# Layers 2 and 3 of a graph network: the row tile that ten blocks share, split once into kept halves

## The chip, the core and the metric

The kernel runs on one core of one Trainium2 chip. The time is the device time of one execution in microseconds (us); lower is better. TensorE is called PE in the views, VectorE DVE, ScalarE ACT, GpSimd POOL, and SyncE SP.

## What is computed

A graph network of 6250 nodes with 256 features and 100,000 edges `src -> dst`, sorted by `dst`. Three layers of the same form, a residual sum and a layer norm:

```
deg  = in-degree + 1 (a self loop on each node);  dinv = 1/sqrt(deg)
for W, b in ((W1, b1), (W2, b2), (W3, b3)):      # 256 -> 512 -> 512 -> 256
    h = relu( segment_sum( (h @ W)[src] * dinv[src] * dinv[dst], dst ) + b )
out  = layernorm(x + h)
```

Each `segment_sum` runs over the edges and the self loops. All data is float32.

## The kernel before, in words

The nodes are cut into 50 blocks of Q = 125. A layer needs, for each block, the sum over its edges of rows of a table (`tab0` for layer 1, `tab1`, 512 wide, for layer 2, `tab2`, 256 wide, for layer 3; they hold the scaled node values and lie in HBM). The code numbers the layers i = 0, 1, 2.

A block's sum is made in one of two ways. A **gathered** block has 16 chunks of 128 edges. For each chunk GpSimd issues an indirect DMA that brings 128 rows of the table into SBUF (line 1159), and PE multiplies them by a 0/1 matrix `shot` that says which row belongs to which node of the block (line 1186). Blocks 22 to 49 are gathered in layer 1, blocks 12 to 49 in layer 2 (38 blocks), blocks 29 to 49 in layer 3 (21 blocks). A **dense** block is made by a product of a matrix of edge counts with the whole table (line 1242 in layers 1 and 3, line 1014 ahead of time; in layer 2 `teams` multiplies four dense blocks at once, line 957).

A block may have more edges than 16 chunks hold. The excess of ten blocks goes into one extra tile of 128 rows, the **shared row tile**, gathered once per ten blocks (the items with `b is None`). Its 17th column of `shot` picks a block's part. So each gathered block ends with a 17th product, of the shared tile, behind its 16th chunk.

For PE, a float32 row tile is split into two halves of the type float32r: ACT copies the row (line 1213, the high half), DVE subtracts the copy from the row (line 1216, what is left), and PE multiplies both. In layer 2 a half is 512 columns, so a chunk is two products of 512 columns; in layer 3 a half is 256 columns, the two lie side by side, and a chunk is one product of 512 columns. The shared tile is not split: it is multiplied as float32 in every block. `product` (lines 1162 to 1196) issues these; the list `several` holds the chunk's halves and, at the block's last chunk, the shared tile from `of_ten`.

The order is written out by hand (`tc.manual_schedule()`), one pass of the loop at line 1203 per chunk. In pass `chunk` stand: the gather of `chunk` (line 1208), ACT's copy of chunk - `hi_lag`, DVE's subtraction of chunk - `lo_lag`, the product of chunk - `lag`, then steps of what follows a block (`after1`, `after2`, `after3`), then dense work. `SPLIT` (line 54) sets the lags: 1, 2 and 8 passes in layer 2, 3, 4 and 9 in layer 3. Every engine runs its own list in order, so a wait holds up all that stands behind it on that engine.

Buffers go round in rings. The raw rows of a layer are a list `rows`; its first two are the two shared tiles (line 1141) and the others a ring that the gathers use in turn: 7 in layer 2 (each 128x512), 17 in layer 3. A raw row is free again when DVE has subtracted. The split rows are a queue `split`: 9 of its own in layer 2 and 3 lent ones (`loaned`, which lie in the space of `parts`, so that the trace shows them as `parts`), 11 in layer 3. A split row goes back to the queue when its product stands (line 1192). Near the end of the teams' work the lent ones aren't put back, and `lag` goes down from 8 to 6.

`after2` turns a finished sum of layer 2 into rows of `tab2`: DVE scales the sum (line 1308), PE transposes it, ACT copies it out (line 1326), PE multiplies by W2 (line 1352), ACT applies the bias and relu (line 1363), PE multiplies by W3 (line 1372), DVE scales (line 1385), SP stores into `tab2` (line 1388, through the helper's line 73). This is done for two blocks at a time. Layer 3's first gather needs the last of these stores. In layer 3 the dense counts are fetched from HBM (`fetch`, through the helper's line 75) into the space `room`, of which the first part also holds raw rows of layer 2, the shared ones among them. `after3` adds the bias and x, takes the norm and stores the output.

Of the kernel before, what the change touches and what calls it, by code (L numbers as in the profile page):

```python
# [10 lines left out]
F32 = mybir.dt.float32  # L11
# [21 lines left out]
LATE = 6  # L33
# [362 lines left out]
def sorted_path(ctx: ExitStack, tc: tile.TileContext, x, edges, starts, found, wts, biases, room, late, out):  # L396
# [14 lines left out]
    nc = tc.nc  # L411
# [22 lines left out]
    rest = const.tile([P, NG, 2], I32, name="rest")  # L434
# [313 lines left out]
    def split_rows_of(stack, name, i, width):  # L748

        pool = stack.enter_context(tc.tile_pool(name=name, bufs=1))  # L750
        return deque(pool.tile([P, 2 * width], F32R, name=f"halves{n}") for n in range(SPLIT_ROWS[i]))

    split = split_rows_of(one, "sfirst_split", 0, C)
# [269 lines left out]
    def fetch(b, chunk):  # L1023
        by_rows(nc.sync, used[len(there) % 2].rearrange("p k v -> p (k v)"), kept[b])
        there.append(chunk)
# [5 lines left out]
    def layer(i, width, gathered, dense, after, rows, first=0, spacing=1.0, extras=(), filler=None, carried=None):  # L1031
# [29 lines left out]
        def go_fixed(chunk):  # L1061
            for item in list(fixed):
                if item[0] <= chunk:
                    wait = next(item[1], None)
                    if wait is None:
                        fixed.remove(item)
                    else:
                        item[0] = chunk + wait

        def go(chunk):  # L1070
            for item in list(going):
                if item[0] <= chunk + late:
                    wait = next(item[1], None)
                    if wait is None:
                        going.remove(item)
                    else:
                        item[0] = chunk + late + min(wait, item[2])
# [8 lines left out]
        def sum_bank(name, most):  # L1086
            nonlocal late
            if i == 0:
                while not common:
                    if early_copy[0]():  # L1090
                        break
                    late += 1
                    go(chunk)
                return common.popleft()
            need(now, name, most)
            return idle[name].pop(0)

        def ended(chunk, b, acc, bank="acc"):

            most = LATE if chunk < total - 2 * KF else 1  # L1100
            going.append([chunk + late + min((3, SOON, LATE)[i], most), after(b, acc, bank), most])
            for item in going:
                item[2] = most
# [4 lines left out]
        def more_hots():  # L1108
            c0 = len(hots) * HOTS
            n = min(HOTS, len(gathered) * (KF + 1) - c0)  # L1110
            if n > 0:
                at = gathered[0] * (KF + 1) + c0
                hot = onehot.tile([P, HOTS, Q], F32R, name="shot")
                nc.vector.tensor_tensor(hot[:, :n], near_cols[:, :Q].unsqueeze(1).to_broadcast([P, n, Q]),  # L1114
                                        dlo.rearrange("p b j -> p (b j)")[:, at:at + n].unsqueeze(2).to_broadcast([P, n, Q]),
                                        op=ALU.is_equal)
                hots.append(hot)

        def converted(m, c):
            piece = pieces.tile([Q, PIECE, Q], F32R, name="piece")  # L1120
            convert = nc.vector.tensor_copy if i == 2 and c % 4 == 1 else nc.scalar.copy
            made_or_read = place_of[dense[m]] if i == 0 else used[m % 2] if m else made
            convert(piece, made_or_read[:, c * PIECE:(c + 1) * PIECE, :])  # L1123
            return piece
# [5 lines left out]
        def of_both(c):  # L1130

            n, b, _ = items[c]
            return i == 0 and (n * GRP if b is None else b) >= BOTH_FROM

        def halved(c):

            return 0 <= c < total and items[c][1] is not None and i > 0
        acc = None

        of_ten = {}  # L1140
        shared, rows = rows[:2], rows[2:]

        def gather(c):
            nonlocal turn
            n, b, j = items[c]
            table = both_halves if of_both(c) else tables[i]
            if (i, b, j) == (0, BOTH_FROM, BOTH_LAG + 1):
                hot_stores.appendleft(late_hot_room)
            if b is None:
                row, at = split.popleft() if of_both(c) else shared[n % 2], rest[:, n, 0:1]  # L1150
                of_ten[n] = row
            elif of_both(c):
                row, at = split.popleft(), src[:, b, j:j + 1]
                split_rows[c] = row
            else:
                row, at = rows[turn % len(rows)], src[:, b, j:j + 1]
                (landed if i > 0 else split_rows)[c] = row
                turn += 1
            nc.gpsimd.indirect_dma_start(out=row, out_offset=None, in_=table,  # L1159
                                         in_offset=bass.IndirectOffsetOnAxis(ap=at, axis=0))  # L1160
# [39 lines left out]
        with tc.manual_schedule():  # L1200
            more_hots()
            to_sum = 0
            for chunk in range(total + (SHORT if i == 1 else lag)):
                now = chunk
                if i == 1:
                    lag = SPLIT[i][2] if returning is None else max(SHORT, SPLIT[i][2] - (chunk - returning) // 2)
                if chunk < total:
                    gather(chunk)
                if halved(chunk - hi_lag):
                    halves = split_rows[chunk - hi_lag] = split.popleft()  # L1210
                    if i == 1 and halves in loaned:
                        on_loan.append(halves)
                    nc.scalar.copy(halves[:, :width], landed[chunk - hi_lag])  # L1213
                if halved(chunk - lo_lag):
                    halves = split_rows[chunk - lo_lag]
                    nc.vector.tensor_sub(halves[:, width:], landed.pop(chunk - lo_lag), halves[:, :width].bitcast(F32))  # L1216
                while to_sum <= chunk - lag:
                    product(to_sum)
                    to_sum += 1
                go(chunk)  # L1220
                go_fixed(chunk)
                until = min(len(dense) * NB, begun + int((chunk + 1 - first) * NB / spacing))
                if i == 0:
                    until = min(until, done + 3)
                if chunk >= total - 1:
                    until = len(dense) * NB
                while done < until:
                    m, k = divmod(done, NB)
                    if k == 0:
                        if chunk < total - 1 and (len(there) <= m or there[m] > chunk):  # L1230
                            break
                        assert len(there) > m
                        acc_d = sum_bank(bank, 3)
                        if i == 2 and m + 1 < len(dense) and len(there) == m + 1:
                            fetch(dense[m + 1], chunk)
                    if k % PIECE == 0:
                        while len(got) < min(len(dense) * CUTS, done // PIECE + 1 + ahead):
                            n, c = divmod(len(got), CUTS)
                            if n > m and (len(there) <= n or there[n] > chunk):
                                break  # L1240
                            got.append(converted(n, c))
                    nc.tensor.matmul(acc_d[:Q], lhsT=got[done // PIECE][:, k % PIECE, :], rhs=parts[:, k],  # L1242
                                     start=(k == 0), stop=(k == NB - 1))
                    products = done = done + 1
                    if k == NB - 1:
                        finished += 1
                        ended(chunk, dense[m], acc_d, bank)
            assert all(steps_ is carried for _, steps_ in fixed)
            while going:
                late += 1  # L1250
                go(chunk)
                if carried is not None:
                    next(carried)
                if filler is not None:
                    next(filler, None)
            while filler is not None and begun % PIECE:
                next(filler)
# [214 lines left out]
    split = split_rows_of(two, "swide_split", 1, HID)  # L1472
# [11 lines left out]
    split = split_rows_of(ctx, "ssplit", 2, C)  # L1484
    spacing = (steps(MANY) - 14) / (MANY - begun / NB)
    layer(2, C, every[MANY:], many, after3, last_rows, 4, spacing)


# [179 lines left out]
```

## Time and profile before

| what | value |
|---|---|
| median of 3 runs | 2101.11 us (2099.72 to 2102.96) |
| the profiled execution's own time | 2099.83 us |
| its span, first to last instruction | 2098.2 us |
| mean granted TensorE clock in it | 0.982 |
| HBM read and written | 415.75 MB, 67.46 MB (230 GB/s over the span) |
| layer 1's gathers / layer 2's / layer 3's | 451 / 612 / 339 (1402 indirect DMAs in all; layer 2 and 3 with 4 and 3 shared tiles) |
| first gather of layer 2 / of layer 3 | at 709.2 us / at 1647.2 us of the span |

The durations in the views are of this one execution. A matmul of two float32 operands shows as two MATMUL records, one of float32r operands as one; both print as `f32`. Matmuls overlap in the pipeline, so the time that one costs in a stream is the distance from its start to the next one's start, not its own duration. In the groups of lines a row ends with busy time, mean duration of one and the idle time of the engine just before them.

### The profile page before, as it was taken

The page shows a single profiled execution, that of the slowest core. Times are in us where ns is not written, and L with a number is a line of the kernel's source. Part 1 is how long each engine was busy: PE and PEld are TensorE (multiplying, and loading weights), DVE is VectorE, ACT ScalarE, POOL GpSimd, SP SyncE. Part 2 cuts the span into 40 slices and gives each one's busy share as a digit, 9 for nine tenths or more (in the row PEclk, how much of TensorE's full clock was granted, in tenths as well). Part 3 has the DMA queues.
Part 4 walks back from the last instruction along what each step waited for, and adds up shares of the span by engine and source line. Part 5 has one row for each costly group of instructions (what it writes and reads, how often), then busy time and mean ns, then how long its engine had stood idle before and what let it go on. Part 6 is the DMA issues. An engine that isn't in the chain of part 4 may idle for free.

```text
span 2098.2 us, 30149 instructions
## 1 busy us (share of the span) xinstructions
PE 1948.5 (93%) x8711; PEld 1518.5 (72%) x8711; DVE 1492.8 (71%) x2822; ACT 1307.4 (62%) x2497; POOL 1421.2 (68%) x1442
## 2 busy tenths in 40 slices
PE   3499999999998789999999999999989899999997
PEld 3377777777776567878878777788767787887775
DVE  5887888888882466776667776577775367777777
ACT  1566777787784466666667666667565456555554
POOL 2467777766777376767667776577775477777775
PEclk9999999999999899999999999999999999999998
DMA  7797999999999999988889898799886376767674
GB/s 167 238 285 231 267 263 255 276 261 260 270 276 256 266 258 254 273 232 247 236 237 268 255 264 226 219 257 264 248 238 192 103 185 181 192 176 192 175 188 120
DMA packets 232032, 485.37 MB, mean 231 GB/s; under 512 B 42937, under 2 KB 85769, under 8 KB 231857
## 3 DMA queue, kind: packets, MB, share of 16 engines
q0 software_dynamic: 125184, 315.61, 54.2%
q1 hardware_dynamic: 90833, 155.90, 26.7%
q10 hardware_dynamic: 15840, 11.86, 2.3%
q8 instruction: 70, 1.15, 0.2%
q14 instruction: 105, 0.86, 0.1%
HBM read 415.75 MB, written 67.46 MB: 230 GB/s over the span
## 4 chain that ended last, share of the span: by engine, by line
PE 67%; DMA 10%; issue 7%; DVE 5%; POOL 4%; ACT 3%; ACTq 0%; SPq 0%; DVEq 0%; POOLq 0%
PE sacc L1186 14%; DMA room<-tab,ssrc 9%; PE win_ps L1352 6%; PE smm L1242 5%; PE win_ps L1242 5%; PE mat_ps L1242 5%; PE sacc L1242 5%; POOL room L1159 4%; PE win_ps L1372 3%; PE sacc L957 2%; PE mat_ps L957 2%; PE str L957 2%; PE smm L957 2%; PE sacc L1289 2%; PE str L1242 2%
## 5 line engine op out<-in xcount | busy, mean ns | idle before, releaser
L1159 POOL DMA_INDIRECT room<-tab,ssrc x1008 | 1028.3, 1020 | 403.3 <-issue 157.2
L1216 DVE TENSOR_TENSOR halves<-room,halves 128x512 fp32r<-128x512 f32 (+1 forms) x818 | 460.4, 579 | 295.1 <-ACT halves L1213 274.7
L1213 ACT CAST halves<-room 128x512 fp32r<-128x512 f32 (+1 forms) x818 | 417.8, 531 | 299.3 <-DMA room<-tab,ssrc 243.8
L1186 PE MATMUL sacc<-halves,shot 128*125 128x512 f32 x1468 | 509.2, 407 | 11.5 <-DVE shot L1114 5.6
L1159 POOL DMA_INDIRECT halves<-both,ssrc x384 | 360.5, 939 | 141.7 <-issue 42.9
L783 DVE TENSOR_TENSOR room<-near_cols,slots 128x625 bf16<-128x625 f32 (+2 forms) x435 | 324.9, 802 | 28.5 <-PE sacc L850 12.2
L1186 PEld LDWEIGHTS sacc<-halves,shot 128*125 128x125 f32 x1468 | 275.4, 189 | 88.4 <-ACT halves L1213 6.6
L1123 ACT CAST piece<-room 125x625 fp32r<-125x625 uint8 x416 | 297.7, 723 | 65.4 <-DVE halves L1216 26.1
L1114 DVE TENSOR_TENSOR shot<-near_cols,sdlo 128x500 fp32r<-128x500 f32 x371 | 247.3, 667 | 9.7 <-PE sacc L1186 5.2
L1352 PE MATMUL win_ps<-room,w_sb 128*128 128x250 f32 (+1 forms) x832 | 190.1, 371 | 14.0 <-ACT room L1326 6.7
L1242 PE MATMUL win_ps<-parts,piece 125*125 125x512 f32 x650 | 186.8, 406 | 5.0 <-ACT piece L1123 4.9
L1242 PE MATMUL smm<-parts,piece 125*125 125x512 f32 x655 | 190.0, 407 | 1.3 <-ACT piece L1123 0.7
L1352 PEld LDWEIGHTS win_ps<-room,w_sb 128*128 128x128 f32 x832 | 154.5, 192 | 42.1 <-ACT room L1326 8.2
L1242 PE MATMUL mat_ps<-parts,piece 125*125 125x512 f32 x600 | 173.1, 406 | 0.4 <-ACT piece L1123 0.4
L850 PEld LDWEIGHTS <-room 128*125 128x125 bf16 x725 | 95.7, 138 | 73.7 <-issue 22.7
L1242 PE MATMUL sacc<-parts,piece 125*125 125x512 f32 x450 | 146.6, 430 | 0.9 <-ACT piece L1123 0.9
L1242 PEld LDWEIGHTS win_ps<-parts,piece 125*125 125x125 f32 x650 | 119.3, 188 | 35.9 <-ACT piece L1123 6.3
L812 ACT CAST room<-sacc 125x500 uint8<-125x500 f32 (+1 forms) x155 | 107.7, 713 | 51.3 <-PE sacc L850 50.9
L1242 PEld LDWEIGHTS smm<-parts,piece 125*125 125x125 f32 x655 | 116.8, 187 | 29.1 <-issue 2.3
L1242 PEld LDWEIGHTS mat_ps<-parts,piece 125*125 125x125 f32 x600 | 108.0, 187 | 27.2 <-issue 2.8
L919 DVE TENSOR_TENSOR parts<-parts 125x512 fp32r<-125x512 f32 x150 | 103.1, 687 | 33.9 <-ACT parts L917 33.7
L957 PE MATMUL sacc<-parts 125*125 125x512 f32 x300 | 106.0, 433 | 13.4 <-ACT parts L917 11.8
(311 smaller groups left out, 3003.3 us busy)
## 6 DMA issues: line engine op xcount, KB each, us to landing
parts<-tab SPq DMA_DIRECT2D x81, 448.0 KB
kept<-room SPq DMA_DIRECT2D x29, 683.6 KB
room<-kept SPq DMA_DIRECT2D x29, 683.6 KB
room<-tab,ssrc POOLq DMA_INDIRECT x1008
tab<-st SPq DMA_DIRECT2D x62, 224.0 KB
both<-parts SPq DMA_DIRECT2D x10, 1120.0 KB
own_row<-tab SPq DMA_DIRECT2D x38, 224.0 KB
parts<-kept SPq DMA_DIRECT2D x60, 136.7 KB
```

The source lines that it names most:

```text
L783: nc.vector.tensor_tensor(out, near_cols[:, :shape[2]].unsqueeze(1).to_broadcast(shape), numbers.unsqueeze(2).to_broadcast(shape), op=ALU. ...
L812: nc.scalar.copy(place[:, :, u * G:(u + len(ms)) * G].rearrange("p k (t r) -> p t k r", r=G), counted_in[:Q, :len(ms) * 256].rearrange("p ...
L919: nc.vector.tensor_sub(to[:, HID:], row, to[:, :HID].bitcast(F32))
L957: nc.tensor.matmul(team_banks[n][:Q], lhsT=team_pieces[(g * CUTS + k // PIECE) % 2][n][:, k % PIECE, :], rhs=both_parts[u % 3][:, h * HID: ...
L1114: nc.vector.tensor_tensor(hot[:, :n], near_cols[:, :Q].unsqueeze(1).to_broadcast([P, n, Q]), dlo.rearrange("p b j -> p (b j)")[:, at:at + ...
L1123: convert(piece, made_or_read[:, c * PIECE:(c + 1) * PIECE, :])
L1159: nc.gpsimd.indirect_dma_start(out=row, out_offset=None, in_=table, in_offset=bass.IndirectOffsetOnAxis(ap=at, axis=0))
L1186: nc.tensor.matmul(acc[:Q, :size], lhsT=hot, rhs=row[:, c0:c0 + size], start=(i == 1 and k == c0 == 0), stop=(k == KF and c0 + size == row ...
L1213: nc.scalar.copy(halves[:, :width], landed[chunk - hi_lag])
L1216: nc.vector.tensor_sub(halves[:, width:], landed.pop(chunk - lo_lag), halves[:, :width].bitcast(F32))
L1242: nc.tensor.matmul(acc_d[:Q], lhsT=got[done // PIECE][:, k % PIECE, :], rhs=parts[:, k], start=(k == 0), stop=(k == NB - 1))
L1352: nc.tensor.matmul(h_ps[:, f, :], lhsT=w2_sb[:, k, (f2 + f) * P:(f2 + f + 1) * P], rhs=zt2[:, k, :wide], start=(k == 0), stop=(k == KH - 1))
```

## The change

In layers 2 and 3 one raw row is kept for shared tiles where there were two, and the one left over joins the ring of raw rows (8 in layer 2, 18 in layer 3). One split row is taken out of `split` for the length of the layer: `shared_halves`. Once per ten blocks, ACT copies the shared tile into its first half and DVE subtracts into the second, 6 to 8 passes behind the gather of the tile and not before the last product of the ten blocks before it stands. The blocks' 17th products then read `shared_halves`: two float32r products of 512 columns in layer 2, one in layer 3. `product` is unchanged. Layer 1 is unchanged.

```
-        shared, rows = rows[:2], rows[2:]
+        shared, rows = rows[:2 if i == 0 else 1], rows[2 if i == 0 else 1:]
+        shared_halves = split.popleft() if i > 0 else None
+        raw_of_ten = deque()
...
             if b is None:
-                row, at = split.popleft() if of_both(c) else shared[n % 2], rest[:, n, 0:1]
+                row, at = split.popleft() if of_both(c) else shared[n % len(shared)], rest[:, n, 0:1]
                 of_ten[n] = row
+                if i > 0:
+                    of_ten[n] = shared_halves
+                    raw_of_ten.append((c, row))
...
                 while to_sum <= chunk - lag:
                     product(to_sum)
                     to_sum += 1
+                if raw_of_ten and to_sum >= raw_of_ten[0][0] and chunk >= raw_of_ten[0][0] + LATE:
+                    row = raw_of_ten.popleft()[1]
+                    nc.scalar.copy(shared_halves[:, :width], row)
+                    nc.vector.tensor_sub(shared_halves[:, width:], row, shared_halves[:, :width].bitcast(F32))
                 go(chunk)
                 go_fixed(chunk)
```

In the built program the lists of PE, ACT and DVE stand in the same order as before but for the replaced products and the seven added copies and subtractions (four in layer 2, three in layer 3); GpSimd's list is the same. On SP one pair of DMAs moves: near the end of layer 2, a fetch of dense counts (`room<-kept`) stands ahead of two stores into `tab2` that it stood behind.

## The prediction

> **What bounds the kernel now.** I read the page first (busy shares, then the chain that ended last), then the stretches of layers 2 and 3, then GpSimd's waits in each.
>
> ```profile
> PE 1948.5 (93%) x8711; PEld 1518.5 (72%) x8711; DVE 1492.8 (71%) x2822; ACT 1307.4 (62%) x2497; POOL 1421.2 (68%) x1442
> ...
> PE 67%; DMA 10%; issue 7%; DVE 5%; POOL 4%; ACT 3%; ACTq 0%; SPq 0%; DVEq 0%; POOLq 0%
> ```
>
> PE is busy 93% and holds 67% of the chain, so taking work from PE should pay. But that is a mean over stages. The columns of the next view are the stretch, its length, busy time of PE, PEld, DVE, ACT, POOL, the granted clock, DMA share and GB/s:
>
> ```profile
> 735.00:1470.00 735.00, 711.59 (x3108) 570.28 (x3107) 513.80 (x824) 476.60 (x877) 513.68 (x495) 0.99 0.89 249
> 1470.00:1580.00 110.00, 95.35 (x411) 75.34 (x410) 82.82 (x134) 68.20 (x127) 80.36 (x79) 0.95 0.86 244
> 1580.00:1647.00 67.00, 65.93 (x322) 53.92 (x321) 29.81 (x55) 31.45 (x66) 22.52 (x23) 0.98 0.49 142
> 1647.00:2085.00 438.00, 425.61 (x1803) 335.83 (x1801) 316.47 (x848) 246.81 (x578) 334.86 (x339) 0.98 0.67 177
> ```
>
> The first three are layer 2, the last is layer 3. PE looks full in all but the second. What GpSimd waits for, in 740 to 1470 us and then in 1647 to 2085 us (total, times, longest), with its gathers in each stretch (min/median/max ns, first and last start), parts them:
>
> ```profile
> L1159 POOL DMA_INDIRECT room<-tab,ssrc x488: 940/946/3287, 740.2 to 1469.0; - x163
> ...
> POOL room L1159 <- DVE halves L1216: 90.5, 108, 4.8
> POOL room L1159 <- DVE parts L1216: 18.9, 29, 3.1
> ```
>
> ```profile
> L1159 POOL DMA_INDIRECT room<-tab,ssrc x336: 942/947/1399, 1648.4 to 2084.7; - x168
> ...
> POOL room L1159 <- issue: 32.9, 108, 0.3
> POOL room L1159 <- DVE halves L1216: 22.5, 74, 0.3
> ```
>
> In layer 2 GpSimd is held back: 109.4 us behind DVE's subtractions, up to 4.8 us at a time. It wants a raw row that is not free yet, because all behind it waits for PE; its gathers come every 728.8/487 = 1.50 us. In layer 3 no wait is over 0.3 us, whatever name stands there: that is the gap between two gathers, and 0.947 + 0.3 = 1.25 us is the engine's own pace. It goes on so from 1648.4 to 2084.7, 436.3/335 = 1.30 us each. So **layer 3 lasts as long as its gathers take to issue**, however full PE is; dense products merely fill PE. The end of the chain agrees: the last gather, its landing, and PE's last products.
>
> ```profile
> 2083.47 0.95 POOL room L1159
> ...
> 2084.73 2.93 DMA room<-tab,ssrc
> ...
> 2088.65 1.66 PE sacc L1186 x3
> ```
>
> **The change part by part.** *The shared products, layer 2.* On the chain of waits a block's end reads (start, length, what):
>
> ```profile
> 766.36 0.47 PE mat_ps L957 x2
> 766.82 1.35 PE sacc L1186 x4
> ...
> 1467.62 0.46 PE sacc L957 x2
> 1468.08 1.33 PE sacc L1186 x4
> ```
>
> The four are the last chunk's two halves and the two records of the float32 shared product; a float32r pair takes 0.47 us in the same chain, so the shared product takes 1.33 - 0.47 = 0.86 us. Afterwards it is a float32r pair, 0.47 us. Saved: **0.39 us a block**. All 38 blocks would give 14.8 us of PE time. But only what lies on the path counts. Of the 38, 24 stand on the chain before 1480 us as such a row (the two rows quoted are the first and the last), and two more after 1579 us; the other 12 fall where the chain runs through gathers. 24 x 0.39 = **9.4 us**, and 2 x 0.39 = **0.8 us**.
>
> Between 1473 and 1577 us the chain is on GpSimd and its landings; there the saving of four blocks buys nothing.
>
> ```profile
> 1472.28 0.67 DVE szs L1308
> ...
> 1473.12 0.48 POOL room L1159
> ...
> 1495.09 9.19 DMA room<-tab,ssrc
> ```
>
> *The shared products, layer 3.* In the order of time around a block's end:
>
> ```profile
> 1701.53 0.40 PE L1186 MATMUL sacc<-halves,shot 128*125 128x512 f32 x1
> 1701.76 0.59 PE L1186 MATMUL sacc<-room,shot 128*125 128x256 f32 x2
> 1702.00 1.28 PE L1242 MATMUL win_ps<-parts,piece 125*125 125x512 f32 x4
> 1703.13 0.40 PE L1171 MATMUL sacc<-parts,ident_r 125*125 125x512 f32 x1
> ```
>
> From 1701.76 to 1703.13 are 1.37 us; four float32r products at 0.23 us (1701.53 to 1701.76) take 0.93, which leaves 0.44 for the shared product. It becomes one float32r product: 0.21 us saved a block, 4.4 us in 21. By the argument above this is worth **nothing**: PE would only catch up with gathers that come no sooner. The one exception is the last block's product, in the quoted 1.66 us, which run at half the clock: twice 0.21, **0.4 us**.
>
> ```profile
> 2088.00:2098.00 10.00, 1.94 (x4) 0.82 (x3) 3.20 (x9) 0.43 (x2) 0.00 (x0) 0.50 0.07 19
> ```
>
> *One more raw row.* Rings of 8 and 18 instead of 7 and 17. In layer 3 GpSimd never waits for a row: nothing. In layer 2 the wait named DVE above is that for a row, and with 8 it asks for a subtraction one chunk older. Where the chain passes from PE to GpSimd's run (1473.12), GpSimd would be one gather further: **1.25 us**. It could do the same at earlier stalls; the 735 us stretch has 23.4 us of PE idle, of which I bound the gain by 0 and a third, 8 us, and take 0, since a shorter stall leaves the other paths in place.
>
> *One split row less* (12 to 11, and 9 to 8 at the end). ACT's copies already wait for PE at times; the second row is for the next paragraph:
>
> ```profile
> ACT halves L1213 <- PE sacc L1186: 16.7, 17, 2.8
> ...
> DVE szs L1308 <- PE sacc L1186: 27.1, 15, 3.5
> ```
>
> Seventeen waits, when ACT is a whole ring ahead of PE. Being a chunk less ahead costs nothing while PE has eleven rows ready; bounds 0 and 17 x 1.50 = 25 us, of which I take 0, because PE itself is what ACT waits for.
>
> *Seven splits.* The rows are one ACT copy and one DVE subtraction of a layer 2 chunk:
>
> ```profile
> L1213 ACT CAST halves<-room 128x512 fp32r<-128x512 f32 x482 | 289.8, 621 | 192.6 <-DMA room<-tab,ssrc 146.9 <-PE sacc L1186 18.3 <-issue 11.3
> L1216 DVE TENSOR_TENSOR halves<-room,halves 128x512 fp32r<-128x512 f32 x482 | 324.7, 691 | 180.1 <-ACT halves L1213 160.1 <-DMA room<-tab,ssrc 11.2 <-PE sacc L1186 6.5
> ```
>
> Four of 0.62 and 0.69 us, three in layer 3 of half the width and no dearer: under 4.4 us of ACT, 4.9 of DVE. ACT is busy 477 of 735 us, DVE 514: their idle time hides it. Without that cover it is 0.6 to 1.3 us each. Five of the seven also bring **a new wait**: ACT's copy may not overwrite the halves until PE has done the last product of the ten blocks before, issued in the same pass. Behind it on ACT stand the next chunks' copies, relus (L1363) and copies of transposes (L1326); on DVE the subtraction, then `shot`. PE has seven chunks' halves ready then, some 10 us of work, and DVE waits for that same product anyway a little later (the second row above, 15 times, up to 3.5 us). I take 0, and bound it by 5 x 3.5 = 17.5 us.
>
> *SP.* The fetch of counts that moves waited for the last shared product, whose raw row it overwrites; it no longer does:
>
> ```profile
> 1622.47 1.59 SPq L73 DMA_DIRECT2D tab<-st  x4
> 1629.40 0.75 SPq L75 DMA_DIRECT2D room<-kept  x2
> ...
> 1644.42 0.76 SPq L73 DMA_DIRECT2D tab<-st  x2
> ```
>
> It now stands ahead of stores that went at 1622.47. If it waits a few us for the last subtractions, those slip, but layer 3 needs the store of 1644.42, 22 us later: nothing.
>
> **The sum:** 9.4 + 0.8 + 0.4 + 1.25 = 11.85 us off. From the profiled execution's 2099.83 this gives 2088.0; that one lies 1.3 below the median of 2101.11, so as a median **2089 us**.
>
> **The rivals.** *PE is the bound everywhere*: 14.8 + 4.4, and the raw row takes up to 8 us of stalls: 19 to 27 off, 2074 to 2082. For it: PE's 67% of the chain, which runs through PE in the first part of layer 3 too. Against it: GpSimd's 0.3 us. A halfway form (all of layer 2's blocks, some stalls, nothing in layer 3) gives 15 to 20 off, 2081 to 2086.
>
> *The gathers take it back in layer 2 too*: GpSimd is at 1.50 us a chunk and could do 1.25, but DMA is at 0.89 of its time with landings of 9 us (1495.09). If the next path lies a few tenths under PE's, at most a third of the 11.85 arrives: 2097 to 2100.
>
> *Slower: stalls at half clock.* A stall of 2.48 us, in the order of time, and the stretch from its end on:
>
> ```profile
> 924.08 3.64 PE L1352 MATMUL win_ps<-room,w_sb 128*128 128x250 f32 x8 [2.48 <-ACT room L1326]
> ```
>
> ```profile
> 924.10:927.50 3.40, 3.40 (x9) 2.81 (x9) 3.10 (x6) 3.40 (x7) 2.46 (x3) 0.51 0.80 196
> ```
>
> After the stall PE ran 3.4 us at half the clock, 1.7 us lost on top. If ACT's new waits and the shorter split ring leave copies of transposes and relus late, each such place costs 2.5 + 1.7 = 4.2 us. Three undo the 11.85; the five new waits, all hit, give 21 off the other way, 2110; four give 2106. It decides once ACT is less than two passes ahead of PE when it meets the wait. The Trainium skill ("TensorE: Matmul & The Clock Gate", section "Why this matters for your kernels") says that gaps of more than about 3 us send the clock to half; by that rule a 2.5 us stall would cost no clock and the price would be 2.5 us a place. Here 2.48 us sufficed, so the trace decides for the dearer one.
>
> *The change doesn't do what it says*: that the new products cost no less than float32. The same PE record already runs 1468 times at the price I use; next to nothing.
>
> **How the numbers follow.** Forecast (2085 to 2093) 0.46; halfway or PE everywhere (under 2085) 0.20; gathers take it back (2093 to 2101) 0.24; slower than 2101 0.10. The range that leaves out two in ten is 2079 to 2099: it covers the forecast, most of the two beside it, and the 8 us bound of the stalls. A measurement of this kernel can tell about 0.2% (4.2 us) from no change, so faster means under 2096.9: 0.46 + 0.20 + half of the 0.24 = 0.78; slower, over 2105.3, 0.08; the rest, 0.14, is the same.
>
> **What would show it.** The chain's block end in layer 2 should read 0.93 us instead of 1.33, and layer 3's shared product one record of 0.23. Layer 2's 38 block ends should come 9 to 11 us earlier by 1480 us. Layer 3 should still take 436 us from first to last gather; if it got shorter by some 4 us, my step on GpSimd's pace is wrong. GpSimd's 109 us behind DVE should fall; if it does but PE's idle time in layer 2 grows by as much as PE saves, the second rival is right. More stretches at half clock, with stalls that end on L1326 or L1363 just behind a new copy, would show the third.

## The result, and the profile after

| | kernel before | changed kernel |
|---|---|---|
| median of 6 runs on one chip | 2102.27 us (2099.72 to 2113.01) | 2087.11 us (2084.82 to 2092.08) |
| ratio, 95% interval | | 0.9923 [0.9898, 0.9949] |
| the profiled execution's span | 2098.2 us | 2090.2 us |
| layer 2's first gather to layer 3's first | 937.9 us | 924.0 us |
| layer 3's first gather to its last | 437.6 us | 440.5 us |

The change takes about 16 us off, with 11 to 21 in the interval; the forecast was 2089 us. The gain is layer 2's; layer 3 has none. First the busy times and the engines' shares of the chain, from the page of the changed kernel:

```profile
PE 1933.4 (92%) x8690; PEld 1513.7 (72%) x8690; DVE 1498.9 (72%) x2829; ACT 1308.7 (63%) x2504; POOL 1426.0 (68%) x1442
...
PE 63%; DMA 13%; DVE 6%; issue 6%; ACT 4%; POOL 3%; ACTq 0%; DVEq 0%; POOLq 0%; SPq 0%
```

PE is 15.1 us less busy (1948.5 before); the 38 and 21 cheaper products would make 14.8 + 4.4 = 19.2. But its share of the chain went from 67 to 63%, and that of the transfers from 10 to 13%: a first hint that the landings of transfers now end the waits more often. Next, layer 2 as one stretch, before and after (columns as in the prediction's first view):

```profile
709.00:1647.00 938.00, 889.41 (x3897) 712.05 (x3896) 638.87 (x1032) 589.04 (x1091) 633.55 (x612) 0.98 0.86 243
```

```profile
712.90:1636.90 924.00, 875.12 (x3896) 712.93 (x3895) 642.55 (x1036) 589.29 (x1095) 636.69 (x613) 0.98 0.88 246
```

The length less PE's busy time is PE's idle time: 48.6 us before, 48.9 after. This looks as if PE's saving had simply gone through to the end. The experiments show that it didn't: the equal sum hides two opposite parts. The two prices that I had worked out do stand in the trace. On the chain, a block's end in layer 2 is 0.93 us where it was 1.33:

```profile
841.37 0.47 PE str L957 x2
841.83 0.93 PE sacc L1191 x4
842.76 0.47 PE sacc L957 x2
```

In layer 3 the last chunk's product and the shared one together take 1691.96 - 1691.49 = 0.47 us, in the order of time on PE:

```profile
1691.49 0.63 PE L1191 MATMUL sacc<-halves,shot 128*125 128x512 f32 x2
1691.96 1.09 PE L1251 MATMUL win_ps<-parts,piece 125*125 125x512 f32 x4
```

GpSimd's waits in the changed kernel, 740 to 1470 us, and its gathers and waits in layer 3:

```profile
POOL room L1164 <- DVE halves L1221: 68.0, 88, 4.4
POOL room L1164 <- DVE parts L1221: 17.8, 27, 2.9
POOL room L1164 <- ACT halves L1218: 8.0, 3, 4.5
```

```profile
L1164 POOL DMA_INDIRECT room<-tab,ssrc x336: 942/947/1394, 1638.1 to 2077.4; - x168
```

```profile
POOL room L1164 <- issue: 34.1, 112, 0.3
POOL room L1164 <- DVE halves L1221: 20.7, 68, 0.3
```

In layer 2 the wait for a subtraction fell from 109.4 to 85.8 us, and a new one came, 8.0 us in three stops behind ACT. In layer 3 the gathers still come every 439.3/335 = 1.31 us, and behind the first of them GpSimd has no wait over 0.3 us: they set its pace, and cheaper products buy nothing there.

### The profile page after: what moved, and what is told of

It reads as the page before. It is cut to its first block, busy times and chain, and to the rows that moved or that the text cites. A ratio compares the mean times of both kernels' runs of the same rounds, so it can differ in the third digit from the quotient of the medians.

```text
span 2090.2 us, 30060 instructions
## 1 busy us (share of the span) xinstructions
PE 1933.4 (92%) x8690; PEld 1513.7 (72%) x8690; DVE 1498.9 (72%) x2829; ACT 1308.7 (63%) x2504; POOL 1426.0 (68%) x1442
## 4 chain that ended last, share of the span: by engine, by line
PE 63%; DMA 13%; DVE 6%; issue 6%; ACT 4%; POOL 3%; ACTq 0%; DVEq 0%; POOLq 0%; SPq 0%
PE sacc L1191 13%; DMA room<-tab,ssrc 12%; PE win_ps L1361 7%; PE sacc L1251 5%; PE smm L1251 4%; PE win_ps L1251 4%; PE mat_ps L1251 4%; PE win_ps L1381 3%; POOL room L1164 3%; PE mat_ps L957 2%; PE sacc L957 2%; PE str L957 2%; DVE halves L1221 2%; PE smm L957 2%; PE sacc L1298 2%
## 5 line engine op out<-in xcount | busy, mean ns | idle before, releaser
L1221 DVE TENSOR_TENSOR halves<-room,halves 128x512 fp32r<-128x512 f32 (+1 forms) x806 | 453.3, 578 | 275.5 <-ACT halves L1218 269.4
L1218 ACT CAST halves<-room 128x512 fp32r<-128x512 f32 (+1 forms) x806 | 409.9, 529 | 269.3 <-DMA room<-tab,ssrc 194.2
L1191 PE MATMUL sacc<-halves,shot 128*125 128x512 f32 x1541 | 525.8, 407 | 13.8 <-DVE shot L1114 7.0
L1191 PEld LDWEIGHTS sacc<-halves,shot 128*125 128x125 f32 x1541 | 289.6, 189 | 95.7 <-DVE shot L1114 11.5
L1221 DVE TENSOR_TENSOR parts<-room,parts 128x512 fp32r<-128x512 f32 x138 | 93.5, 692 | 38.2 <-ACT parts L1218 37.5
```

The source lines that it names most:

```text
L1191: nc.tensor.matmul(acc[:Q, :size], lhsT=hot, rhs=row[:, c0:c0 + size], start=(i == 1 and k == c0 == 0), stop=(k == KF and c0 + size == row ...
```

## The experiments

The theory of the prediction: on PE's path 24 cheaper products in layer 2 pay 9.4 us, the additional raw row about one gather (1.25 us), ACT's new wait nothing. The main rival: the raw row pays, and the products' saving is taken back by the gathers or by the new wait. All ratios are to the kernel before on the same chip.

### The two parts apart, and the two layers apart

`e1`, the kept halves with the ring back at seven raw rows (17 in layer 3):

```
-        shared, rows = rows[:2 if i == 0 else 1], rows[2 if i == 0 else 1:]
+        shared, rows = rows[:2], rows[2:]
```

> The changed kernel, but with two raw rows set aside as before, so layer 2's ring of raw rows stays at 7 (layer 3's at 17); the kept halves and the cheaper products stay. My theory (PE time on the path, 24 + 2 blocks of 0.39 us and 0.4 at the end) expects 10.6 us less than before, within 3 us, so a few us short of the change. The rival (the raw row is what pays) expects under 4 us.

`e2`, the shared product in float32 as before, with eight raw rows; the second shared tile lies in the space of a split row, so that the split ring is one shorter, as in the changed kernel:

```
-        shared, rows = rows[:2], rows[2:]
+        if i == 0:
+            shared, rows = rows[:2], rows[2:]
+        else:
+            shared, rows = [rows[0], split.popleft()[:, :width].bitcast(F32)], rows[1:]
```

> The kernel before with one raw row more in the ring (8 and 18) and one split row less, as in the change, but the shared tile still multiplied as float32 in every block (its second raw place lies in the split row). My theory expects 1 to 2 us less than before. The rival (the raw row pays) expects 8 us or more; the rival that the shorter split ring costs expects more time than before.

`e3` and `e4`, the whole change in layer 2 alone and in layer 3 alone:

```
+        kept_once = i == 1        # e4: i == 2
+        shared, rows = rows[:1 if kept_once else 2], rows[1 if kept_once else 2:]
+        shared_halves = split.popleft() if kept_once else None
...
-                if i > 0:
+                if kept_once:
```

> The change in layer 2 alone; layer 3 as before. My theory expects all of the change's gain but 0.4 us. The rival (PE is the bound everywhere) expects 4.4 us less gain than the change.

> The change in layer 3 alone; layer 2 as before. My theory (layer 3 lasts as long as its gathers take to issue) expects 0.4 us less than before and 436 us from layer 3's first to last gather, as before. The rival (PE is the bound everywhere) expects 4.4 us less.

Measured: e1 0.9998 [0.9972, 1.0024], e2 0.9966 [0.9946, 0.9987], e3 0.9973 [0.9952, 0.9994], e4 1.0015 [0.9992, 1.0038]. But the kernel before took 2360.11 us on this chip, 12% more than on the first, so these say little about the first result. What is different there is seen in GpSimd's, ACT's and DVE's order of time, here from `e9` below, which ran on a third chip of the same kind (before: 2356.52 us):

```profile
2148.70 0.95 POOL L1164 DMA_INDIRECT room<-tab,ssrc  x1 [0.30 <-issue]
2149.95 0.95 POOL L1164 DMA_INDIRECT room<-tab,ssrc  x1 [0.30 <-issue]
2154.82 0.95 POOL L1164 DMA_INDIRECT room<-tab,ssrc  x1 [3.92 <-DVE halves L1221]
```

```profile
2153.08 0.72 ACT L1123 CAST piece<-room 125x625 fp32r<-125x625 uint8 x1 [7.23 <-remote]
```

```profile
2153.11 0.49 DVE L1123 CAST piece<-room 125x625 fp32r<-125x625 uint8 x1 [6.46 <-remote]
```

About every 20 us GpSimd, ACT and DVE stand still together for 3 to 7 us, while PE's matmuls come 0.7 to 1.4 us apart instead of 0.23. Between the stops the gathers keep their 1.25 us; with them layer 3's gathers take 521 to 527 us instead of 437 to 441. What stops the engines the profile doesn't name ("remote"). The order e2, e3, e1, e4 fits the rival, but most of the intervals overlap: only e2's and e4's lie apart, and only just (0.9987 and 0.9992).

### The same on a chip without the stops

> The changed kernel as it is, on the chip of this call, as the measure for the three beside it. Theory and rivals: 10 to 16 us less than before where the kernel before takes about 2100 us.

> The kept halves with a ring of 7 raw rows (17 in layer 3), once more, beside the change. In the first call the kernel before took 2360 us, all engines paused together in its traces, and this kernel brought nothing; I expect it to bring 8 to 11 us less than before where there are no such pauses, and the change 1 to 5 us more. If it brings under 4 us there too, the raw row is what pays, and my sum had the wrong term.

> Eight raw rows (18 in layer 3), one split row less and float32 products, once more, beside the change. It brought 8 us on the first chip. My theory expects 1 to 4 us less than before where there are no pauses; the rival (the raw row pays) 8 or more.

`e8` is the changed kernel, but the split waits for six more chunks' products; by then the last product of the ten blocks before is long done:

```
-                if raw_of_ten and to_sum >= raw_of_ten[0][0] and chunk >= raw_of_ten[0][0] + LATE:
+                if raw_of_ten and to_sum >= raw_of_ten[0][0] + 6 and chunk >= raw_of_ten[0][0] + LATE:
```

> The changed kernel, with the split of the shared tile put six chunks later, so that ACT no longer waits for a product that PE was given in the same pass. In the changed kernel's profile ACT waits 9.0 us there in layer 2, and GpSimd's gathers stop for 4.5 us behind one of these waits. If that costs time on the path, this is 2 to 5 us faster than the change; if PE hides it (as I predicted), it is within 1 us of the change and only the wait is gone.

Before took 2103.71 us here. Ratios with their intervals, and medians:

| layer 2's ring | shared product float32 | kept halves |
|---|---|---|
| 7 raw rows | 1 | e6: 1.0009 [0.9992, 1.0026], 2104.26 us |
| 8 raw rows | e7: 0.9926 [0.9902, 0.9950], 2090.39 us | e5: 0.9930 [0.9910, 0.9949], 2089.27 us |
| 8, split six chunks later | | e8: 0.9889 [0.9861, 0.9917], 2083.04 us |

This settles the main question. **The raw row alone brings the whole gain; the cheaper products alone bring nothing, and beside the raw row nothing that stands out of the noise either** (0.9930 against 0.9926, each within about 0.2%). Without the early split they seem to bring 6.2 us more (e5's median to e8's), but the two intervals overlap a little. Layer 2 as a stretch in e6, e7, e5 and e8:

```profile
715.30:1649.80 934.50, 879.05 (x3897) 714.25 (x3896) 641.74 (x1036) 591.14 (x1095) 642.24 (x613) 0.98 0.86 243
```

```profile
713.50:1637.70 924.20, 884.71 (x3897) 711.07 (x3896) 638.42 (x1032) 587.65 (x1091) 646.37 (x613) 0.98 0.87 246
```

```profile
713.40:1640.00 926.60, 878.98 (x3896) 715.42 (x3895) 641.82 (x1036) 590.18 (x1095) 645.95 (x612) 0.98 0.87 245
```

```profile
711.30:1630.10 918.80, 874.12 (x3897) 712.42 (x3896) 640.02 (x1036) 588.15 (x1095) 636.03 (x613) 0.98 0.88 248
```

These are single executions, and before was traced on the first chip. The two of the changed kernel (924.0 us long with 875.1 busy above, 926.6 with 879.0 here) differ by 2.6 and 3.9 us, so differences of that size can't be read. One example: in its trace e6's layer 2 is 3.4 us shorter than before's, but its layer 1, whose code is the same, is 6.1 us longer (715.3 instead of 709.2), and the medians show no gain.

PE's idle time is 48.6 us before, 55.5 with the halves alone (e6), 39.5 with the raw row alone (e7), 47.6 with both (e5), 44.7 with both and the later split (e8). The halves take 10.4 us of busy time away and give 6.9 back as idle (before to e6); beside the raw row it is 5.7 and 8.1 (e7 to e5). The raw row takes 9.1 and 7.8 us of idle time away (before to e7, e6 to e5).

*What takes the saving back.* The shares of the chain of waits by line, 722 to 1470 us, before, e6, e7 and e8:

```profile
by line: PE sacc L1186 23.3%; PE win_ps L1352 13.9%; DMA room<-tab,ssrc 11.6%; issue 8.7%; PE win_ps L1372 6.5%; POOL room L1159 6.2%; PE mat_ps L957 5.7%; PE sacc L957 5.6%; PE str L957 5.6%; PE smm L957 5.5%; ACT halves L1213 1.3%; PE sac
```

```profile
by line: PE sacc L1191 22.5%; PE win_ps L1361 15.5%; DMA room<-tab,ssrc 13.3%; PE win_ps L1381 6.9%; issue 6.5%; PE mat_ps L957 5.8%; PE smm L957 5.7%; PE sacc L957 5.7%; PE str L957 5.7%; POOL room L1164 3.9%; PE sacc L1272 1.0%; ACT halve
```

```profile
by line: PE sacc L1189 28.5%; PE win_ps L1355 16.3%; DMA room<-tab,ssrc 7.8%; PE win_ps L1375 7.4%; PE mat_ps L957 6.6%; PE smm L957 6.6%; PE str L957 6.6%; PE sacc L957 6.6%; issue 4.7%; POOL room L1162 2.3%; PE sacc L1266 1.4%; ACT parts 
```

```profile
by line: PE sacc L1191 23.3%; PE win_ps L1361 15.5%; DMA room<-tab,ssrc 10.8%; PE win_ps L1381 7.6%; issue 7.4%; PE sacc L957 6.1%; PE str L957 6.0%; PE mat_ps L957 6.0%; PE smm L957 5.9%; POOL room L1164 4.7%; PE sacc L1272 1.3%; ACT parts 
```

Read the third item of each. The landings of gathers hold 11.6% of the chain before; cheaper products raise that to 13.3% (as I read it, PE comes sooner to rows that have not landed), an eighth row lowers it to 7.8%. Layer 2 is bound by PE and by the landings in turn. ACT's waits for landings in the whole of layer 2 say the same, first before, then e7:

```profile
ACT halves L1213 <- DMA room<-tab,ssrc: 146.9, 124, 4.2
...
ACT parts L1213 <- DMA room<-tab,ssrc: 28.7, 23, 2.6
```

```profile
ACT halves L1216 <- DMA room<-tab,ssrc: 99.8, 86, 3.7
...
ACT parts L1216 <- DMA room<-tab,ssrc: 23.0, 21, 2.6
```

In sum 175.6 us before and 122.8 in e7; with the halves 163.2 at seven rows (e6), 120.4 at eight (e5). The row takes some 43 to 53 us of these waits away, the halves 2 to 12.

*Where the time goes.* The start of a gather in layer 2, in us after the layer's first gather, from the gathers' records:

| gather | before | e6 | e7 | e5 | e8 |
|---|---|---|---|---|---|
| 128 | 184.6 | 182.4 | 176.6 | 178.0 | 178.8 |
| 160 | 232.6 | 231.4 | 218.8 | 222.5 | 223.4 |
| 288 | 429.2 | 428.2 | 415.8 | 415.9 | 417.4 |
| 320 | 475.1 | 474.0 | 459.4 | 463.9 | 459.9 |
| 448 | 672.2 | 670.8 | 659.5 | 662.1 | 657.0 |
| 480 | 718.8 | 717.8 | 704.9 | 709.1 | 700.5 |
| 608 | 898.7 | 895.0 | 882.0 | 884.9 | 877.1 |

The raw row's gain is made early: 13.8 of its 16.7 us by gather 160. That stretch before and in e7:

```profile
709.20:941.80 232.60, 208.75 (x860) 162.61 (x859) 160.55 (x254) 146.53 (x267) 164.81 (x160) 0.95 0.91 260
```

```profile
713.50:932.30 218.80, 202.50 (x849) 159.19 (x848) 159.33 (x251) 145.09 (x262) 164.10 (x160) 0.95 0.97 275
```

The DMA engines go from 0.91 to 0.97 busy, 260 to 275 GB/s, and PE idles 16.3 instead of 23.9 us: with one more row in flight the transfers run closer together. On e7's own chip e6, with seven rows, has 0.92 and 262 GB/s in this stretch, and e5, with eight, 0.97 and 271. (PE also did fewer matmuls in e7's, 849 instead of 860.) The stall that I had quoted from before, PE at 924.08 waiting for ACT's L1326, shows it on the chain of waits, followed back:

```profile
912.42 9.84 DMA room<-tab,ssrc
...
922.33 0.56 ACT halves L1213
...
923.46 0.58 ACT room L1326
...
924.08 3.64 PE win_ps L1352 x8
```

The copy that PE waited for stood on ACT behind the copy of a gathered row that took 9.84 us to land. A row asked for one gather earlier should land earlier: in e7 PE's waits for this copy are 0.5 us in the same stretch from 722 us on, in before 4.8.

*What the new wait costs.* e5 loses against e8 in two places: from gather 288 to 320 it takes 48.0 us, e8 42.5, and from 448 to 480 47.0 against 43.5 (the first profiled run of the changed kernel: 49.1 and 48.0). There stand two of the three waits at L1227 that layer 2 shows; the first of the three, near gather 140, costs nothing visible. In e5 and in the first profiled run, in the order of time on ACT:

```profile
1149.19 0.62 ACT L1227 CAST halves<-room 128x512 fp32r<-128x512 f32 x1 [1.75 <-PE sacc L1191]
...
1157.53 0.62 ACT L1218 CAST halves<-room 128x512 fp32r<-128x512 f32 x1 [2.68 <-DMA room<-tab,ssrc]
...
1161.29 0.62 ACT L1218 CAST halves<-room 128x512 fp32r<-128x512 f32 x1 [2.67 <-DMA room<-tab,ssrc]
...
1165.37 0.62 ACT L1218 CAST halves<-room 128x512 fp32r<-128x512 f32 x1 [2.94 <-DMA room<-tab,ssrc]
```

```profile
1396.85 0.62 ACT L1227 CAST halves<-room 128x512 fp32r<-128x512 f32 x1 [5.46 <-PE sacc L1191]
```

On GpSimd, just behind each:

```profile
1152.48 0.95 POOL L1164 DMA_INDIRECT room<-tab,ssrc  x1 [2.13 <-ACT halves L1218]
1153.73 1.90 POOL L1164 DMA_INDIRECT room<-tab,ssrc  x1 [0.31 <-DVE parts L1221]
1155.93 3.29 POOL L1164 DMA_INDIRECT room<-tab,ssrc  x1 [0.30 <-issue]
```

```profile
1399.55 0.94 POOL L1164 DMA_INDIRECT room<-tab,ssrc  x1 [4.52 <-ACT halves L1218]
```

ACT stands at L1227, the copies of the next chunks stand behind it, so raw rows come free late and GpSimd stops, 2.1 and 4.5 us. A few us later ACT waits for landings one after the other. In e5 PE then stalls, and from 1174 us on it runs at about half the clock for 3.6 us:

```profile
1173.07 2.64 PE L1361 MATMUL win_ps<-room,w_sb 128*128 128x250 f32 x8 [1.88 <-ACT room L1372]
```

```profile
1174.00:1177.60 3.60, 3.60 (x10) 2.85 (x9) 2.56 (x4) 3.60 (x8) 2.68 (x4) 0.53 0.98 291
```

In e8 no copy at L1227 waits for PE (its engine sat idle before it: no entry). That the two places lost 9.0 us to e8 is measured in one pair of runs; that the wait's stop is the cause is read from the order of events, and e8, where only the wait's place differs, agrees. It is not shown to be the whole cause. At the first place two gathers right behind the stop took 1.90 and 3.29 us instead of 0.95 each, 3.3 us more; the first profiled run has the same two, e8 none between gathers 288 and 320, and what slows single gathers no run shows. And with seven rows the wait seems to cost nothing: e6 has it three times too (2.42, 1.94 and 1.69 us), and takes 45.8 and 47.0 us for the two stretches, where before takes 45.9 and 46.6.

### Where is the next bound? Runs that could not tell

Four more kernels went to the third chip, with the stops. `e9` is e1 with the later split, `e11` before with `rows[3:]` in layer 2. The other two are e8 with these edits:

```
         shared_halves = split.popleft() if i > 0 else None
+        if i == 1:                                             # e10
+            two_more = split.popleft().bitcast(F32)
+            rows = rows + [two_more[:, :width], two_more[:, width:]]
...
+                if i == 1 and k == KF:                         # e12, in product
+                    continue
...
-                                     stop=(k == KF and c0 + size == row.shape[1]))
+                                     stop=(k == (KF - 1 if i == 1 else KF) and c0 + size == row.shape[1]))   # e12
```

So e10 has ten raw rows and ten split ones in layer 2, and e12 leaves the shared product out there.

> The kept halves with the split six chunks later, but the raw ring back at seven rows in layer 2 (17 in layer 3). Theory A (two gains beside each other: the eighth row pays about 15 us by itself, and the cheaper products pay about 8 us as soon as ACT's new wait is gone; with the early split the wait ate the 8): about 8 us under before, ratio 0.996, and ACT's wait on PE at L1227 is absent. Theory B (seven raw rows are the bound of layer 2, cheaper products pay only behind an eighth row): no difference from before, ratio 1.000, and what PE saves turns into PE waiting for the subtractions. Theory C (the later place of the split helps for its own sake and the products count for nothing): also 0.996, but then a kernel with less work for PE gains nothing either.

> The late split, and one split row of layer 2 more given up for two more raw rows: ten raw rows, ten split rows. If the raw ring still limits the gathers behind the eighth row, GpSimd's waits for the subtractions fall by another third at least and the kernel is 5 to 15 us under the late split with eight rows (2083): 2068 to 2078. If PE sets the pace with eight rows already, within 3 us of 2083. If ten split rows are too few now, ACT's waits for PE at L1218 grow and it is above 2083, up to 2095.

> The kernel before with six raw rows in layer 2 instead of seven; all else untouched. If the number of raw rows sets how far the landings of the gathers are covered (theory A and B), one row less costs more than the eighth gained: 15 to 40 us over before, 2118 to 2143, GpSimd's wait for the subtractions grows well over 90 us, and so do ACT's waits for landings. If the eighth row only helped by the place where it lies or by a changed order of waits, six rows cost little: under 5 us.

> The late split with eight rows, and layer 2 leaves out the product of the shared row tile in all its 38 blocks (so the excess edges are missing from the sums of layer 2): 38 x 0.47 = 17.9 us less of PE's work, nothing else changed. If PE is what layer 2 waits for with eight rows (theory A): 12 to 18 us under the late split, 2065 to 2071. If the gathers are (theory B, with the eighth row just enough for the cheaper products): 0 to 5 us under it, and PE's idle time grows by the rest. Theory C: 0.

Measured: e9 0.9966 [0.9941, 0.9991], e10 0.9983 [0.9962, 1.0005], e11 0.9989 [0.9963, 1.0014], e12 0.9974 [0.9950, 0.9997]. e9 gives the number that theories A and C both name, and e11 came out at its second expectation (a row counts for little). But neither can be taken over to the chip without the stops: on the chips with the stops, 18 us less of PE's work (e12), an eighth row (e2) and only six rows (e11) all stay within 0.35% of before, with intervals that overlap. So these times tell no theory from another. The mechanism of the rows can be read in the traces all the same. ACT's waits for landings in the whole of layer 2, with 6 rows (e11), 7 (e4), 8 (e2) and 10 (e10):

```profile
ACT halves L1213 <- DMA room<-tab,ssrc: 107.9, 81, 5.8
...
ACT parts L1213 <- DMA room<-tab,ssrc: 27.7, 24, 3.8
```

```profile
ACT halves L1219 <- DMA room<-tab,ssrc: 72.6, 53, 3.7
...
ACT parts L1219 <- DMA room<-tab,ssrc: 23.1, 19, 2.6
```

```profile
ACT halves L1216 <- DMA room<-tab,ssrc: 30.9, 23, 3.1
...
ACT parts L1216 <- DMA room<-tab,ssrc: 17.4, 11, 2.3
```

```profile
ACT halves L1221 <- DMA room<-tab,ssrc: 12.3, 12, 2.3
...
ACT parts L1221 <- DMA room<-tab,ssrc: 11.1, 6, 5.8
```

In sum 135.6, 95.7, 48.3 and 23.4 us: every row takes some 12 to 47 us (24.9 / 2 from 8 to 10, 47.4 from 7 to 8) of waiting for landings off ACT. The rows are not all that differs: e2 and e10 have fewer split rows, and e10 also has the kept halves. On these chips it doesn't show in the time of the program.

## Why the prediction came out near, and which steps of it failed

The time was 2087 against 2089 us, but that was luck: two errors nearly cancel, 10.6 us of products that didn't come and a raw row worth 14 us more than its 1.25.

- **"24 x 0.39 = 9.4 us" (with 0.8 and 0.4).** The 0.39 is right (0.93 instead of 1.33 us), the step from it to the end is wrong. e6 has all of these products and takes 1.0009 of the time, with at most 0.08% (1.7 us) of gain in its interval. I counted rows on the chain and took their saving as the program's; but a row on the chain pays only as far as the next path lies below. This was my own second rival, "the gathers take it back in layer 2 too", at 0.24.
- **"One more raw row: 1.25 us", bounded by 8 for earlier stalls.** This is the term that was mis-sized most: e7 measures 0.9926, 15.6 us (10 to 21). (The medians, 2103.71 and 2090.39, lie 13.3 apart.) I had read GpSimd's 109 us as "all behind it waits for PE" and looked for the row's gain only where the chain enters GpSimd's run. The stalls of PE that go with it were in the trace, and the one I quoted came from a landing, two steps back on the chain.
- **"Seven splits … a new wait … I take 0".** Probably wrong by much of what the products could bring: some 6 us by the medians, 9.0 by the two places, inside the bound of 17.5. I argued that PE had "some 10 us of work" ready and that ACT was ahead. It isn't PE that starves at the wait, it is GpSimd: the gathers behind the stop land late some ten us afterwards. This is the third rival's mechanism in part (late copies at two places, a stall of PE at the first), outweighed by the raw row. Its half clock came in one trace of two: in e5 a stall of 1.88 us was followed by 3.6 us at a granted clock of 0.53; in the first profiled run the stall at the same place, 2.24 us, was followed by the full clock. The Trainium skill ("TensorE: Matmul & The Clock Gate", section "Why this matters for your kernels") puts the limit at gaps of about 3 us. Stalls of 1.88 and 2.48 us that cost clock lie under it; but the length alone doesn't decide, and the 4.2 us that the prediction puts on every such place are too much for some. In the kernel before itself, a stall of 2.29 us on the same line was followed by the full clock:

```profile
833.70 1.96 PE L1352 MATMUL win_ps<-room,w_sb 128*128 128x250 f32 x8 [2.29 <-ACT room L1326]
```

```profile
833.70:837.10 3.40, 3.40 (x16) 2.98 (x17) 2.71 (x5) 3.40 (x7) 2.18 (x3) 1.00 1.04 295
```

- **Layer 3 worth nothing.** Right: 440.5 us from first to last gather (437.6 before), e6 with cheaper products there 437.2, and no wait of GpSimd over 0.3 us behind the first gather. With 18 raw rows layer 3 takes 438.7 to 440.9 us in four traces (first changed run, e5, e7, e8), with 17 it takes 437.2 and 437.6 (e6, before); what makes these few us was not tried.
- **One split row less, 0.** Not tried by itself: e5 to e8 all have the shorter ring. e7 gains 15.6 us with it, so its cost can't be seen.
- **What would show it.** I had written that gather times 9 to 11 us earlier by 1480 us would speak for my sum; gather 504 does come 10.8 us earlier (739.9 instead of 750.7 us after the first). That was no test: both theories give it (e7, without the cheaper products, is 13.6 us earlier there).

Open: whether cheaper products pay with seven rows once the wait is gone, how much of e8's 6 us is the wait and how much the slow gathers, and whether rows beyond eight still pay, since those runs came on a chip that can't tell. The best kernel measured is e8.

## What to carry to other kernels

A change that frees a buffer beside making an instruction cheaper is two changes: price the buffer by the stalls whose chain goes back to a landing, not by where the chain happens to enter the gathers. Two paths that lie close together take turns, and cutting one pays only until the other; the idle time of a stage (its length less busy time), read for each part of the change alone, shows it. Before a wait is costed at nothing, follow what stands behind it on its engine to the buffers that it frees, and place it where what it waits for is already done.

## What the runs showed of the hardware that was not expected

- The same program takes 12% longer on some chips (2356 to 2360 us against 2102 to 2104): stops of 3 to 7 us on GpSimd, ACT and DVE together, about every 20 us, with the gathers between them 1.25 us apart as elsewhere. The cause is open. In such a run PE idles over 100 us in layer 2 (e12: 1013.8 us long, 894.0 busy), and 26 us less of PE's busy time than in e4 (1020.9 us long, 920.2 busy) makes the layer 7 us shorter.
- One raw row of 128x512 float32 more, 8 instead of 7, raised the DMA engines' busy share from 0.91 or 0.92 (before, e6) to 0.97 (e5, e7) in a stretch where the gathers on the chain took 4.8 to 9.8 us to land (before, 722 to 942 us).
- Whether PE's clock is halved behind a stall doesn't follow from the stall's length alone: 1.88 us (e5, 1173.07) and 2.48 us (before, 924.08) were followed by a granted clock of 0.53 and 0.51, 2.29 us (before, 833.70) and 2.24 us (first changed run, 1171.21) by 1.00.
- Single gathers take up to 3.3 us on GpSimd instead of 0.95. Gathers 305 and 306 of layer 2 took 1.90 and 3.29 us in both traces of the changed kernel, and not in e8. The cause is open.
